# Expert blocks of 192 rows in a Mamba layer with a mixture of experts

## The chip, the core and the metric

The kernel runs on one core of a Trainium2 chip. A core has a matrix engine (TensorE, PE in the profile; its weight loads are listed as PEld), a vector engine (VectorE, DVE), an engine for activation functions (ScalarE, ACT), a general one (GpSimd, POOL), and SyncE (SP), which only issues transfers. They run beside each other and wait for each other through semaphores; 16 DMA engines move the data. Matrix products end in PSUM, which has eight banks of 512 fp32 columns by 128 partitions.

The metric is the time of one execution on the device in microseconds, lower is better. A profiled execution also leaves a trace, from which every duration below is taken.

## What is computed

4096 tokens of 256 numbers go through a Mamba layer, then through a layer in which each token is sent to one of eight experts. Both layers add their input and normalise. The second layer is what the change is about (`attn` stands for the first):

```python
x = _layernorm(x + attn(x, ...), axis=-1)
# D_MODEL, D_FF, N_EXP = 256, 1024, 8
logits = xf @ Wr.T + br
expert_idx = jnp.argmax(logits, axis=-1)
h = jax.nn.relu(jnp.einsum('td,efd->etf', xf, W1) + b1[:, None, :])
y = jnp.einsum('etf,edf->etd', h, W2) + b2[:, None, :]
out = y[expert_idx, jnp.arange(xf.shape[0])]
x = _layernorm(x + out, axis=-1)
```

The reference computes all experts for all tokens and picks one; the kernel computes only the expert that each token chose. All arithmetic of the two expert products is fp32.

## The kernel before

**Stages.** The Mamba layer runs over eight tiles of 512 tokens (`project`, `gauge`, `scan`, `gate`, `project_out`). `choose` and `rank` find each token's expert and its place in that expert's list, and `place` writes its number there (`lists`). The normalised tokens go to a DRAM array `x1d`, one row per token, with a row of zeros behind them.

**Expert blocks.** A block is up to 128 tokens of one expert's list. For block b, `prefetch` has POOL gather its tokens from `x1d` into `xg` (L399) and the expert's whole weights, 2.2 MB, into one of three buffers (L405, `held_weights[b % SLOTS]`), two blocks ahead (`AHEAD`). `turn` transposes the tokens on TensorE (L415), and DVE copies the result to `xgT` (L419). `hidden` computes the hidden layer in two halves, each of four chunks of 128 hidden units into one PSUM bank `ph` (L431); ACT empties the first half with bias and relu (L439), DVE the second (L441), both into `hT`. `close` computes the second product into one bank `pe` (L452), and calls `finish`: DVE adds tokens and bias (`xs`, L465) and the product (`r`, L467) and normalises (`layernorm`, L243 to L250; the square root in it is ACT's, L247). `scatter` has POOL write the rows to their tokens' places in `out` (L473). A row that stands for no token has an index beyond the end and isn't written.

**Tables.** Which expert and which tokens a block has is known only from the data. `table` computes it on DVE, with eight numbers per partition, one for each expert: `whole`, the rows that a list gives to the blocks of this table, then `ends` and `starts` of each list among the blocks, then for every block its place in `lists` (`row`, `pick`) and its expert (`eb`, `widx`). `lookup` fetches the tokens' numbers with a small product (`pi`) into `tidx`. Three early tables, after 3, 5 and 6 tiles, hand out 17 blocks that are full already; the last one, after all eight tiles, hands out the rest. In the last table the blocks are dealt to the three weight buffers in three runs, so that neighbours in a buffer often have the same expert; `same` then marks a load that isn't needed (its index goes out of bounds).

**How many blocks.** At most 39 are possible (`NSB`). `SURE` of them always run, here 37; the remaining two stand in a branch at the end (L940), entered on all engines when the last table's `total` exceeds the 20 blocks that are sure. The branch's condition is loaded into a register of every engine three blocks before the last (L931). Around the branch stand the scatters of the two blocks, from a tile `done` that is zeroed in case they do not run, and `finish` and `scatter` of block 36, which are kept behind it.

**Order.** TensorE's instructions run in the order in which the program writes them (`manual_schedule`, L109): the function `blocks` is a generator that yields after each quarter of a block, and the main loop calls `expert(n)` to run n quarters between the pieces of the Mamba layer. Blocks 0 to 10 or so lie among the last tiles; from then on only blocks run. The instructions of the other engines are ordered by the framework's scheduler, which may move an instruction ahead when what it needs is there. A branch is one unit in this order: on no engine do its instructions mix with others. PSUM's banks are dealt under three names: "mm" (three banks, `ph`), "o" (three, `pe`) and "tr" (two, the transposes).

Of the kernel before, what the change touches and what calls it, by code (L numbers as in the profile page):

```python
# [34 lines left out]
F32 = mybir.dt.float32  # L36
# [9 lines left out]
P = 128  # L46
# [3 lines left out]
TB = 512  # L50
# [11 lines left out]
SURE = 37  # L62
# [7 lines left out]
RUN = -(-(SURE - EARLY[6]) // SLOTS)  # L70
EPS = 1e-5
# [17 lines left out]
def mamba_moe(  # L89
# [148 lines left out]
    def layernorm(pool, rows, n, done, name):  # L238

        mv = pool.tile([P, n, 2], F32, tag="mv", name=f"mv{name}")  # L240
        for j in range(n):
            st = pool.tile([P, 6], F32, tag="st", name=f"st{name}_{j}")
            nc.vector.bn_stats(st, rows[:, j, :])  # L243
            nc.vector.bn_aggr(mv[:, j, :], st)
        sd = pool.tile([P, n], F32, tag="sd", name=f"sd{name}")
        nc.vector.tensor_scalar(sd, mv[:, :, 1], EPS, None, ALU.add)  # L246
        nc.scalar.activation(sd, sd, AF.Sqrt)  # L247
        nc.vector.reciprocal(sd, sd)
        for j in range(n):
            nc.vector.tensor_scalar(  # L250
                done[:, j, :], rows[:, j, :], mv[:, j, 0:1], sd[:, j : j + 1],
                ALU.subtract, ALU.mult,
            )
# [3 lines left out]
    index, weights = {}, {}  # L257
# [3 lines left out]
    held = []  # L261
    r1 = ctx.enter_context(tc.tile_pool(name="r1", bufs=1))
# [7 lines left out]
    def table(b0, nb, columns, rows, early):  # L270
# [5 lines left out]
        def wide(a):  # L276
            return a.unsqueeze(1).to_broadcast([P, nb, NE])
# [12 lines left out]
        nc.vector.tensor_tensor(whole, up, taken, ALU.subtract)  # L290
        ends = small("ends", [NE])
        nc.vector.tensor_tensor_scan(ends, ones8, whole, 0.0, ALU.mult, ALU.add)
        starts = small("starts", [NE])
# [9 lines left out]
        number = blockno[:, 0:nb].unsqueeze(2).to_broadcast([P, nb, NE])  # L303
        past = small("past", [nb, NE])
        nc.vector.tensor_tensor(past, wide(ends), number, ALU.is_le)
        here = small("here", [nb, NE])
        nc.vector.tensor_tensor(here, wide(starts), number, ALU.is_le)
        nc.vector.tensor_tensor(here, here, past, ALU.subtract)
        nc.vector.tensor_tensor(here, here, wide(shift), ALU.mult)
        row = small("row", [nb])  # L310
        nc.vector.tensor_reduce(row, here, AX.X, ALU.add)
        nc.vector.tensor_tensor(row, row, blockoff[:, 0:nb], ALU.add)
        pick = small("pick", [LH, nb])
# [3 lines left out]
        nc.vector.tensor_reduce(eb, past, AX.X, ALU.add)  # L317

        nc.vector.tensor_scalar(eb, eb, float(P), None, ALU.mult)
        if not early:  # L320

# [7 lines left out]
        for b in range(nb):  # L329
            weights[b0 + b] = widx[:, order(b0, b)]  # L330
# [661 lines left out]
```

## Time and profile before

Three runs took 503.46, 504.59 and 505.03 us, median 504.59. The execution that was profiled took 506.53 us, and its span, from the first to the last instruction in the trace, is 504.7 us. The granted TensorE clock averaged 0.995 of full speed.

| what | from the profile |
|---|---|
| hidden layer, L431 | 1184 instructions, 139.9 us busy |
| second product, L452 | 592 instructions, 135.0 us busy |
| transposes of tokens, L415 | 74 instructions, 14.2 us busy |
| evictions of the hidden layer | ACT L439 367 ns, DVE L441 343 ns each, 148 of each |
| one block's y from r on DVE and ACT | L467 423, L243 426, L244 181, L246 153, L247 203, L248 162, L250 433 ns |
| POOL, per issue | tokens L399 978 ns, weights L405 1048 ns, scatter L473 1028 ns |
| issue to landing, median | weights 9.2 us, tokens 4.7 us, scatter 7.1 us |
| engines from 461.97 to 469.22 us | PE 7.25, DVE 3.56, ACT 1.34, POOL 3.00 us busy of 7.25 |
| DMA in three stretches | 294 to 303 us: 381 GB/s; 310 to 346: 339; 418 to 491: 154 |

A fp32 matrix product is two instructions in the trace, so the 16 products of a block's hidden layer are 32. Their listed durations overlap, since matmuls are pipelined; what one really takes is seen in the distance between neighbours, or in the pieces of the chain of waits. That chain is followed back from the last instruction of the run, at each step to what released it; a piece is given as start, length, engine, tile, line and number of instructions. In the groups, "a | b | c" are the total busy time, and the idle time just before on that engine, with what ended most of it.

### The profile page before, as it was taken

How to read it: one execution, taken by the hardware profiler on the slowest of the kernel's cores; microseconds unless marked ns; L12 is line 12 of the kernel's file. 1: busy time of each engine (PE TensorE's matmuls, PEld its weight loads, DVE VectorE, ACT ScalarE, POOL GpSimd, SP SyncE). 2: the span in 40 equal slices, each digit the busy share in tenths (PEclk: the TensorE clock that was granted, in tenths of full speed). 3: DMA queues.
4: the chain of work that ended last, by engine and by line, in shares of the span. 5: the costliest groups of instructions: out<-in, count | busy, mean ns of one | idle time of the engine just before them, and what ended most of it. 6: DMA issues, size and time to landing. Idle time of an engine off the chain costs nothing.

```text
span 504.7 us, 7931 instructions
## 1 busy us (share of the span) xinstructions
PE 490.7 (97%) x2762; PEld 375.9 (74%) x2762; DVE 346.6 (69%) x1130; ACT 223.5 (44%) x472; POOL 184.5 (37%) x189
## 2 busy tenths in 40 slices
PE   7999999999999999999999999999999999999994
PEld 5444555545464586777889999999999999999994
DVE  2587869797999889869889785454545454545443
ACT  3786768777878774844351312211221222122211
POOL 2003022444446445323424233334433443344333
PEclk9998999999999999999999999999999999999999
DMA  7401012120408917507657598899755422811650
GB/s 239 142 1 43 0 43 83 44 83 0 127 1 354 340 29 258 189 0 269 227 202 266 220 359 312 330 363 342 276 201 205 158 97 55 346 54 33 222 192 22
DMA packets 23738, 84.89 MB, mean 168 GB/s; under 512 B 5934, under 2 KB 15665, under 8 KB 20242
## 3 DMA queue, kind: packets, MB, share of 16 engines
q0 software_dynamic: 9360, 69.60, 37.6%
q1 hardware_dynamic: 13378, 14.50, 9.1%
q8 instruction: 23, 0.38, 0.3%
q10 hardware_dynamic: 960, 0.27, 0.3%
q14 instruction: 17, 0.14, 0.1%
HBM read 102.75 MB, written 9.31 MB: 222 GB/s over the span
## 4 chain that ended last, share of the span: by engine, by line
PE 77%; DVE 14%; issue 3%; DMA 2%; ACT 2%; POOL 1%; POOLq 0%; SPq 0%; ACTq 0%
PE ph L431 26%; PE pe L452 25%; PE pm L526 12%; PE po L694 7%; DVE acc L539 5%; DVE cv L653 2%; PE pg L415 2%; PE px L561 2%; DMA xg<-x1d,tidx 1%; PE py L646 1%; DMA xTb<-in_xT 1%; PE pz L794 1%; DVE nma L712 1%; PE pt L620 1%; DVE sta L702 1%
## 5 line engine op out<-in xcount | busy, mean ns | idle before, releaser
L431 PEld LDWEIGHTS ph<-xgT,we 128*128 128x128 f32 x1184 | 138.5, 192 | 4.4 <-issue 1.1
L431 PE MATMUL ph<-xgT,we 128*128 128x128 f32 x1184 | 139.9, 275 | 0.0
L452 PE MATMUL pe<-we,hT 128*128 128x256 f32 x592 | 135.0, 379 | 0.0
L526 PE MATMUL pm<-xTb,win 128*128 128x512 f32 (+1 forms) x260 | 121.3, 597 | 1.3 <-DMA xTb<-in_xT 1.1
L452 PEld LDWEIGHTS pe<-we,hT 128*128 128x128 f32 x592 | 109.4, 190 | 13.6 <-DVE lg L735 0.3
L247 ACT ACTIVATE sdm<-sdm 128x1 f32<-128x1 f32 x37 | 7.5, 203 | 175.2 <-DVE sdm L246 175.2
L405 POOL DMA_INDIRECT we<-in_experts,widx x39 | 40.9, 1048 | 114.8 <-DVE r L467 82.5
L526 PEld LDWEIGHTS pm<-xTb,win 128*128 128x128 f32 x260 | 47.2, 191 | 47.7 <-issue 41.7
L539 DVE SCALAR_TENSOR_TENSOR acc<-xc,cw,acc 128x512 f32<-128x512 f32 x96 | 70.8, 766 | 16.8 <-ACT acc L535 16.4
L441 DVE TENSOR_SCALAR hT<-ph,we 128x128 f32<-128x128 f32 x148 | 42.6, 343 | 39.5 <-PE ph L431 39.5
L694 PE MATMUL po<-wout,sg 128*128 128x264 f32 x256 | 64.4, 393 | 1.3 <-DVE sg L658 1.3
L658 POOL TENSOR_TENSOR sg<-cv,sg 128x512 f32<-128x512 f32 x22 | 33.8, 1539 | 59.5 <-DVE cv L653 44.4
L694 PEld LDWEIGHTS po<-wout,sg 128*128 128x128 f32 x256 | 46.0, 190 | 11.7 <-issue 2.9
L467 DVE TENSOR_TENSOR r<-pe,xs 128x256 f32<-128x256 f32 x37 | 15.7, 423 | 53.2 <-PE pe L452 53.0
L473 POOL DMA_INDIRECT out<-y,tidx x37 | 38.0, 1028 | 38.4 <-DVE y L250 32.1
L399 POOL DMA_INDIRECT xg<-x1d,tidx x39 | 38.2, 978 | 37.6 <-DVE xs L465 9.6
L439 ACT ACTIVATE hT<-ph,we 128x128 f32<-128x128 f32 x148 | 42.1, 367 | 15.7 <-PE ph L431 13.2
L783 POOL TENSOR_SCALAR rowh<-lrow,row,code 128x256 f16<-128x256 bf16 x20 | 25.8, 1300 | 27.4 <-DVE row L775 27.4
L653 DVE SCALAR_TENSOR_TENSOR cv<-cv,dp,py 128x256 f32<-128x256 f32 x64 | 28.9, 470 | 2.4 <-PE py L646 2.4
L531 ACT ACTIVATE sg<-pm 128x512 f32<-128x512 f32 x32 | 19.0, 595 | 18.1 <-PE pm L526 15.8
L533 ACT COPY xc<-pm 128x512 f32<-128x512 f32 x32 | 18.6, 580 | 17.5 <-PE pm L526 17.4
L535 ACT ACTIVATE acc<-pm,cb,cw 128x512 f32<-128x512 f32 x32 | 25.1, 783 | 0.0
(156 smaller groups left out, 477.6 us busy)
## 6 DMA issues: line engine op xcount, KB each, us to landing
xb<-in_x SPq DMA_DIRECT2D x8, 512.0 KB, 4.9
x1d<-x SPq DMA_DIRECT2D x8, 512.0 KB, 5.0
xTb<-in_xT SPq DMA_DIRECT2D x7, 512.0 KB, 3.7
we<-in_experts,widx POOLq DMA_INDIRECT x39, 9.2
xg<-x1d,tidx POOLq DMA_INDIRECT x39, 4.7
out<-y,tidx POOLq DMA_INDIRECT x37, 7.1
win<-in_W_in SPq DMA_DIRECT2D x1, 512.0 KB, 5.7
we<-in_W_outT SPq DMA_DIRECT2D x1, 512.0 KB, 6.2
```

The lines of the kernel that those rows point to most:

```text
L399: nc.gpsimd.indirect_dma_start(out=xgs[n], out_offset=None, in_=x1d[0 : index[n][0], :], in_offset=bass.IndirectOffsetOnAxis(ap=index[n][1 ...
L405: nc.gpsimd.indirect_dma_start(out=wes[n][:, :], out_offset=None, in_=experts, in_offset=bass.IndirectOffsetOnAxis(ap=weights[n], axis=0), ...
L431: nc.tensor.matmul(ph[:, n * P : (n + 1) * P], lhsT=we[:, at : at + P], rhs=xgT[:, dc * P : (dc + 1) * P], start=(dc == 0), stop=(dc == DC ...
L439: nc.scalar.activation(hT[:, fc, :], ph[:, n * P : (n + 1) * P], AF.Relu, bias=bias)
L441: last[b] = nc.vector.tensor_scalar(hT[:, fc, :], ph[:, n * P : (n + 1) * P], bias, 0.0, ALU.add, ALU.max)
L452: nc.tensor.matmul(py[:, 0:D], lhsT=hT[:, fc, :], rhs=we[:, at : at + D], start=(fc == 0), stop=(fc == FC - 1),)
L473: moved = nc.gpsimd.indirect_dma_start(out=out, out_offset=bass.IndirectOffsetOnAxis(ap=index[b][1], axis=0), in_=ys[b][:, 0, :], in_offse ...
L526: nc.tensor.matmul(pm[:, at], lhsT=win[:, dc, c * P : (c + 1) * P], rhs=xTb[:, dc, at], start=(dc == 0), stop=(dc == DC - 1),)
L539: nc.vector.scalar_tensor_tensor(acc, xc[:, c, k : k + TB], cw[:, c, k : k + 1], acc, ALU.mult, ALU.add)
L653: nc.vector.scalar_tensor_tensor(cv[:, c, at], cv[:, c, at], dp[:, c : c + 1], py[:, 0 : TB // 2], ALU.mult, ALU.add,)
L658: eng.tensor_tensor(sg[:, c, :], cv[:, c, :], sg[:, c, :], ALU.mult)
L694: nc.tensor.matmul(po[:, 0 : D + NE], lhsT=sg[:, c, j * P : (j + 1) * P], rhs=wout[:, c, :], start=(c == 0), stop=(c == CC - 1),)
```

## The change

Block 17, 20, 23, 26 and 29, the blocks that one weight buffer gets from the last table, can hold 192 rows (`LONG`). The last table finds up to five experts whose lists end in 1 to 64 tokens beyond a multiple of 128 and have a full block before that; these tokens (`MORE`) go with the list's last full block, which is taken out of the ordinary order (`whole` loses two blocks) and put at the head of the table, where the long blocks are. With no such list, a long block runs as an ordinary one, with indices beyond the end in its further rows.

A long block has a second gather and a second scatter, two more transposes of 64 rows, a hidden layer of 192 columns in four PSUM banks of two chunks instead of two of four, a second product `pf` for the 64 further rows, whose even and odd chunks of hidden units go to two halves of a bank and are added by DVE, and a second `finish`. Its tiles lie in buffers of the Mamba layer that are free by then ("sg" and "xc").

32 blocks always run; the other seven stand in the branch, which moves from the end to between blocks 29 and 30 (`BRANCH`, `seldom`). Their tokens are gathered before the branch, their rows scattered after it, whether it is entered or not. Inside, each of them has its weights loaded by SP into one buffer. Block 30 is turned after the branch instead of during block 29, and block 31's `finish` is no longer held back.

```diff
-SURE = 37
+SURE = 32
...
 RUN = -(-(SURE - EARLY[6]) // SLOTS)
+EXTRA, MORE = 5, 64
+LONG = {EARLY[6] + SLOTS * n: n for n in range(EXTRA)}
+BRANCH = SURE - 2
...
+    def layernorm(pool, rows, done, name):
+
+        n = rows.shape[0]
+        st = pool.tile([P, 6], F32, tag="st", name=f"st{name}")[0:n, :]
+        nc.vector.bn_stats(st, rows)
+        mv = pool.tile([P, 2], F32, tag="mv", name=f"mv{name}")[0:n, :]
+        nc.vector.bn_aggr(mv, st)
+        sd = pool.tile([P, 1], F32, tag="sd", name=f"sd{name}")[0:n, :]
+        nc.vector.tensor_scalar(sd, mv[:, 1:2], EPS, None, ALU.add)
...
+        longer = 0 if early else EXTRA
+        if longer:
+
+            low = small("low", [NE], I32)
+            nc.vector.tensor_scalar(low, pn[:, 0:NE], float(MORE - 1), None, ALU.add)
+            nc.vector.tensor_scalar(low, low, -P, None, ALU.bitwise_and)
+            more = small("more", [NE])
+            nc.vector.tensor_tensor(more, up, low, ALU.subtract)
+            nth = small("nth", [NE])
+            nc.vector.tensor_tensor(nth, low, taken, ALU.is_gt)
+            nc.vector.tensor_tensor(more, more, nth, ALU.mult)
+
+            nc.vector.tensor_tensor_scan(nth, ones8, more, 0.0, ALU.mult, ALU.add)
+            nc.vector.scalar_tensor_tensor(
+                more, nth, float(longer * P), more, ALU.is_le, ALU.mult
+            )
+            nc.vector.tensor_tensor(nth, nth, more, ALU.subtract)
+            base = small("base", [1])
+            nc.vector.tensor_reduce(base, more, AX.X, ALU.add)
+            nc.vector.scalar_tensor_tensor(whole, more, -2.0, whole, ALU.mult, ALU.add)
+
+            key = small("key", [NE])
+            nc.vector.tensor_scalar(key, more, 0.0, float(OFF), ALU.is_equal, ALU.mult)
+            nc.vector.tensor_tensor(key, key, nth, ALU.add)
+            mine = small("mine", [longer, NE])
...
+            row_of = small("row_of", [longer])
+            nc.vector.tensor_reduce(row_of, mine, AX.X, ALU.add)
         ends = small("ends", [NE])
         nc.vector.tensor_tensor_scan(ends, ones8, whole, 0.0, ALU.mult, ALU.add)
+        if longer:
+            nc.vector.tensor_scalar(ends, ends, base, None, ALU.add)
...
+        row = small("row", [nb + longer])
+        nc.vector.tensor_reduce(row[:, 0:nb], here, AX.X, ALU.add)
+        if longer:
+            nc.vector.tensor_tensor(row[:, 0:longer], row[:, 0:longer], row_of, ALU.add)
+            nc.vector.scalar_tensor_tensor(
+                row[:, nb:], row_of, float(P), blockoff[:, 0:longer], ALU.add, ALU.add
...
+            nc.vector.tensor_scalar(
+                spare, eb[0:1, SURE - b0 : NSB - b0], float((NE - 1) * P), None, ALU.min
+            )
...
+            for b, x in LONG.items() if longer else ():
+                further[b] = tidx[0:MORE, nb + x : nb + x + 1]
...
     def prefetch(b):
-        for n in range(b, min(b + AHEAD, NSB - 1) + 1):
+        for n in range(b, min(b + AHEAD, SURE - 1) + 1):
             if n in index and n not in xgs:
                 xgs[n] = m3.tile([P, D], F32, tag="xg", name=f"xg{n}", bufs=4)
-                nc.gpsimd.indirect_dma_start(
-                    out=xgs[n], out_offset=None, in_=x1d[0 : index[n][0], :],
-                    in_offset=bass.IndirectOffsetOnAxis(ap=index[n][1], axis=0),
-                )
+                gather(xgs[n], *index[n])
+                if n in LONG:
+                    ends_[n] = a2.tile([P, CC, KC - 1 + TB], F32, tag="xc", name=f"long{n}")
+                    ends_[n] = ends_[n].rearrange("p c t -> p (c t)")
+                    xgf[n] = ends_[n][0:MORE, 0:D]
+                    gather(xgf[n], index[n][0], further[n])
...
+    def rows_of(b):
+        return P + MORE if b in LONG else P
+
+    def buffer(b):
+
+        if b not in wide_:
+            wide_[b] = a3.tile([P, CC, TB], F32, tag="sg", name=f"wide{b}")
+            wide_[b] = wide_[b].rearrange("p c t -> p (c t)")
+        return wide_[b]
+
     def turn(b):
 
+        n = rows_of(b)
         px = bank("tr", f"pg{b}", 2)
         for dc in range(DC):
-            nc.tensor.transpose(
-                px[:, dc * P : (dc + 1) * P], xgs[b][:, dc * P : (dc + 1) * P], ident
-            )
-        turned[b] = m2.tile([P, DC * P], F32, tag="xgT", name=f"xgT{b}")
-        nc.vector.tensor_copy(turned[b], px[:, 0 : DC * P])
+            at = slice(dc * P, (dc + 1) * P)
+            nc.tensor.transpose(px[:, dc * n : dc * n + P], xgs[b][:, at], ident)
+            if b in LONG:
+                nc.tensor.transpose(
+                    px[:, dc * n + P : (dc + 1) * n], xgf[b][:, at], ident[0:MORE, 0:MORE]
+                )
+        if b in LONG or b >= SURE:
+            turned[b] = buffer(b)[:, FC * n : (FC + DC) * n]
+        else:
+            turned[b] = m2.tile([P, DC * P], F32, tag="xgT", name=f"xgT{b}")
+        nc.vector.tensor_copy(turned[b], px[:, 0 : DC * n])
...
+        per = 512 // P if b not in LONG else 2
+        for first in range(half * FC // 2, (half + 1) * FC // 2, per):
+            ph = bank("mm", f"ph{b}_{first}")
+            for n in range(per):
+                for dc in range(DC):
+                    at = dc * FF + (first + n) * P
+                    nc.tensor.matmul(
+                        ph[:, n * w : (n + 1) * w], lhsT=we[:, at : at + P],
+                        rhs=xgT[:, dc * w : (dc + 1) * w],
+                        start=(dc == 0), stop=(dc == DC - 1),
+                    )
...
-        if half == 0 or b == SURE - 1:
+        if half == 0:
             return
+        if b in LONG:
+
+            openf[b] = bank("o", f"pf{b}")
+            for fc in range(FC):
+                g = fc % 2 * MORE
+                nc.tensor.matmul(
+                    openf[b][g : g + MORE, 0:D], lhsT=hT[:, fc, P:], rhs=out_weights(fc),
+                    start=(fc < 2), stop=(fc >= FC - 2), tile_position=(0, g),
+                )
         finish(b)
...
+        layernorm(m2, r, ys[b], f"m{b}")
+        if b in LONG:
+            xs, r, yf[b] = (ends_[b][0:MORE, n * D : (n + 1) * D] for n in (1, 2, 3))
+            nc.vector.tensor_tensor(xs, xgf[b], we[0:MORE, OC : OC + D], ALU.add)
+            for g in range(2):
+                part_sum = openf[b][g * MORE : (g + 1) * MORE, 0:D]
+                nc.vector.tensor_tensor(r, part_sum, r if g else xs, ALU.add)
+            layernorm(m2, r, yf[b], f"f{b}")
...
+        for rows, at in ((ys[b], index[b][1]), *(((yf[b], further[b]),) if b in LONG else ())):
+            moved = nc.gpsimd.indirect_dma_start(
+                out=out, out_offset=bass.IndirectOffsetOnAxis(ap=at, axis=0),
+                in_=rows, in_offset=None, bounds_check=T - 1, oob_is_err=False,
+            )
...
+    def seldom():
+
+        rows = a3.tile([P, CC, TB], F32, tag="cv", name="rows").rearrange("p c t -> p (c t)")
+        for b in range(SURE, NSB):
+            xgs[b] = ys[b] = rows[:, (b - SURE) * D : (b - SURE + 1) * D]
+            gather(xgs[b], *index[b])
+        with tc.If(held[1] > (SURE - EARLY[6]) * P, preferred_fallthrough_block=False):
+            for b in range(SURE, NSB):
+                wes[b] = held_weights[(BRANCH - 1) % SLOTS]
+                row = nc.values_load(
+                    spare[0:1, b - SURE : b - SURE + 1], engines=[mybir.EngineType.SP],
+                    min_val=0, max_val=(NE - 1) * P,
+                )
+                nc.sync.dma_start(wes[b], experts[bass.ds(row, P), :])
+                turn(b)
+                for half in range(2):
+                    hidden(b, half)
+                for half in range(2):
+                    close(b, half)
...
+        for b in range(SURE):
             current = b
+            if b == BRANCH:
+                seldom()
...
-            if 0 < b < SURE:
+            if 0 < b:
                 scatter(b - 1)
+            if b == BRANCH:
+                for n in range(SURE, NSB):
+                    scatter(n)
             if b not in turned:
                 turn(b)
...
-            if b + 1 in xgs and b + 1 < SURE:
+            if b + 1 in xgs and b + 1 not in (BRANCH, SURE):
                 turn(b + 1)
...
-        if current == SURE - 3 and len(held) == 1:
+        if current == BRANCH - 3 and len(held) == 1:
...
-    done = a2.tile([P, NSB - SURE, D], F32, tag="xb", name="done")
-    nc.vector.memset(done, 0.0)
-    for b in range(SURE, NSB):
-        ys[b] = done[:, b - SURE : b - SURE + 1, :]
-    with tc.If(held[1] > (SURE - EARLY[6]) * P, preferred_fallthrough_block=False):
-        for _ in blocks(SURE, NSB):
-            pass
-    for b in range(SURE, NSB):
-        scatter(b)
-
-    finish(SURE - 1)
     scatter(SURE - 1)
```
`gather` issues the indirect transfer that `prefetch` wrote out before. `mine` and `expert_of`, left out above with three more lines of the table, say which expert a long block has; `hid` of a long block is the first part of `buffer(b)`, and `w` is `rows_of(b)`.

## Prediction

> **What bounds the kernel now.** I read the summary of the page first, then the chain of waits over the last two hundred microseconds, then single blocks in it, and last the timeline of the end.
>
> ```profile
> PE 490.7 (97%) x2762; PEld 375.9 (74%) x2762; DVE 346.6 (69%) x1130; ACT 223.5 (44%) x472; POOL 184.5 (37%) x189
> ...
> PEclk9998999999999999999999999999999999999999
> ```
>
> TensorE is busy nearly all the time at its full clock; DVE is only half used in the last 200 us. A busy share alone does not prove a bound, so the chain of waits between 346 and 360 us is the real evidence:
>
> ```profile
> 346.21 3.57 PE ph L431 x32
> 349.79 0.22 PE pg L415 x2
> 350.00 3.46 PE pe L452 x16
> 353.46 3.57 PE ph L431 x32
> ```
>
> The pieces abut: 3.57 + 0.22 + 3.46 = 7.25 us, and the next block starts at 353.46. No piece of another engine stands between them from 283 us to the last matmul. This expert stage is bound by TensorE alone, so a block less is worth its whole 7.25 us, and a column more costs what TensorE takes for it. Weight loads do not set the pace here: a load is issued at most once per block, lands in 9.2 us (median), and is asked for two blocks (14.5 us) ahead.
>
> **Removed: five blocks.** The loop that always runs goes from 37 to 32. 5 x 7.25 = **-36.2 us**.
>
> **Added: five blocks grow to 192 rows.** Four terms for each, all on TensorE.
> - *Hidden layer.* 32 instructions (an fp32 product is two) now stream 192 columns. For 128 columns one takes 3.57/32 = 0.1116 us; for 256 columns (the second product) 3.46/16 = 0.216 us; for 512 columns (pm, 1.72 us for 4) 0.430 us. The three lie on a line, so 192 columns is the middle of the first two, 0.164 us: 32 x 0.0523 = +1.67 us.
> - *Second product of the 64 further rows (pf).* 16 instructions of 256 columns, in two column groups of 64 (`tile_position`). Unpaired they would cost 3.46 us. The nearest row uses the same two groups:
>
> ```profile
> 192.74 1.72 PE pm L526 x4
> 194.45 1.87 PE px L561 x8
> 196.32 1.98 PE ph L431 x16
> ```
>
> Eight px instructions of 512 columns take 1.87 us where four full-width ones take 1.72, so the groups run beside each other. pf is the same number of streamed columns in twice as many instructions: +1.87 us. Here a rule speaks against the change. The Trainium skill, TensorEngine Tiling (Array Packing), says under Key Properties that a change of tiling mode drains TensorE, and under Restrictions that column tiling switches fast weight load off. If each of the 16 weight loads (137 ns in the px row) stood bare beside 16 x 0.108 us of streaming, pf would be about 3.9 us and the five blocks 10 us dearer. The px row leaves only 1.87 - 1.72 = 0.15 us for drain and loads together, so I take the row; it has half as many loads per column, which is why I keep 3.9 as the upper end.
> - *Transposes.* Two more, of 64 rows; two of 128 take 0.22 us. Between 0.11 and 0.22; I take 0.15.
>
> Sum 3.69 us for a long block, 5 x 3.69 = **+18.5 us**. Net of the two parts: **-17.8 us** (between -19 and -8).
>
> The other work of a long block lies beside TensorE. DVE gets one more sum chain (about 3 us) in a stretch where it works 3.56 of 7.25 us; the chain follows pf and must be through before the next block's L441, which is 3.57 us into that block: it fits. ACT's evictions are 4 x 0.37 us before and little wider now. The four ph banks of a long block rotate through three; the first is emptied 1.5 us before it is needed. POOL issues two more transfers (2 x 1.3 us with their gap); it idles 3.2 us in every block. If one of these covers failed, the cost would be under 1 us a block.
>
> **The last table.** About 24 small DVE instructions of 0.15 to 0.2 us are added, at most 4.8 us of chain. In the trace `pick` is done at 300.16 us (L315), and TensorE takes it up at 305.92 (pi): 5.8 us of cover. The evictions L441 that alternate with the table have 1.3 us of slack before their matmul. I take **0**; without the cover up to +2. The table's tokens are needed only at block 17, which begins near 347 us, 40 us after tidx.
>
> **The branch moves into the stream.** Before, it stands after TensorE's last product and hides there. Now it stands between blocks 29 and 30, and block 29 is a long one. What counts is the DVE queue: all of block 29's ends are before the branch, and `turn(30)`, which is no longer done ahead, is behind it. TensorE cannot start block 30 until DVE has copied xgT. With E as the end of block 29's pe: the chain for one block is read at the end of the trace,
>
> ```profile
> 498.18 0.42 DVE L467 TENSOR_TENSOR r<-pe,xs 128x256 f32<-128x256 f32 x1 [1.49 <-PE pe L452]
> ...
> 499.94 0.41 DVE L250 TENSOR_SCALAR y<-r,mvm,sdm 128x256 f32<-128x256 f32 x1
> ```
>
> that is 2.17 us from r to the end of y, with matmuls ended at 498.14. So block 29's own y is done at E + 2.2; its further rows need one more addition (0.46) and the same chain (2.17): E + 4.9. The branch itself:
>
> ```profile
> L940 DVEq COMPARE_BRANCH  x2: 51/53/55, 494.7 to 496.0; - x2
> ...
> L940 PEldq COMPARE_BRANCH  x2: 95/202/310, 495.9 to 498.3; - x2
> ...
>   DVE xs L465: 0.4, 1
> ```
>
> DVE loses 0.4 us; then xgT 0.41, the hop to TensorE and its first weights 0.2: E + 5.9. TensorE alone would go on at E + 1.87 (after pf) plus 0.22 for the transposes. A gap of **+3.8 us**. TensorE's own branch (0.31 us after its drain, at E + 2) and its transposes are over by E + 3 and lie inside the gap. Lower end 1 us, if the chain of the further rows turns out to run beside something; upper end 7.5.
>
> The upper end comes from a second rule. The Trainium skill, Runtime: NRT & Kernel Launch, Instruction fetch mechanics, says that a taken branch to a target outside the fetched window waits for a DMA of the target page. In the trace the branch jumped past two blocks and the next PE event came within 0.1 us, so no such wait is seen; now seven blocks (some 700 TensorE instructions) lie in between, while the instruction queue's packets are 0.38 MB / 23 = 16.5 KB each. The nearest price is a small transfer's landing, 3.6 us (al, 0.1 KB). On TensorE (ready at about E + 6.5 with xgT then still to come) it would add 1 us; on DVE all 3.6. DVE's body is about 90 instructions, so I take the row, not the rule: no fetch wait.
>
> POOL gathers seven unused blocks' rows before the branch (7 x 1.26 = 8.8 us) and scatters them after it (9 us more). Nothing keeps the gathers from being placed early, into POOL's 3.2 us idle per block, as the memset `done` was (written at the end of the program, run at 272 us). The scatters have 17 us until the last one. Cost **0**; if the gathers are left in a row in front of the branch, from 3.7 us into block 29 on, the last lands 12.5 us later (11.5 us to issue it, 4.7 to land), near E + 7.5, and if the branch's body is waited for, the gap is 6.8 instead of 3.8 us.
>
> SP's, ACT's and the other engines' register loads for the branch move with it (block 27 instead of 34); in the trace TensorE's load at 476.0 us left its period at 7.25. Cost 0. **The end** keeps its form: from the last pe to the end of the span 504.7 - 498.14 = 6.6 us before and after.
>
> **Sum.** -36.2 + 18.5 + 3.8 = -13.9 us. The profiled execution took 506.53 us with a span of 504.7; it would become 492.6 (span 490.8). The shown runs' median, 504.59, lies 1.9 us under that execution, so the forecast for a median is 504.59 - 13.9 = **490.7 us**.
>
> **Rivals.**
> 1. *The gap at the branch is larger* (page fetch, or gathers in front of the branch, or both): +3 to +7 on the sum, 493.5 to 498. For it: 8.8 us of POOL work and a body 3.5 times longer. Against it: slack on POOL and the cheap branch in the trace. 0.22.
> 2. *pf does not pair*, 3.5 to 3.9 us instead of 1.87: 5 x 1.6 to 2.0 us, 499 to 500.7. For it the rule; against it the px row. 0.05.
> 3. *No gap at the branch*: -17.8 + about 1, 487 to 488. For it: nothing but that DVE might be ordered more cleverly. 0.08.
> 4. *Slower: the branch is taken*, and the change does not do what it says. It decides at more than 15 blocks in the last table. Each of seven further blocks then costs 7.25 us, and its weights, all in one buffer and loaded after the block before, 9.2 more: 7 x 16.4 = 115 us, about 606 us. Against it: I counted the reference's choices for its inputs, 495, 560, 487, 548, 514, 589, 514 and 389 tokens. That is 37 blocks of 128; 17 are done early, 20 are left; five lists end in 1 to 64 tokens (48, 36, 2, 2, 5) and each saves one: exactly 15. There is no block to spare, but no list stands where one token changes it for the worse. 0.05, with all other ways to end slower.
>
> The forecast itself, 488.5 to 493.5, has 0.60. The range takes rivals 1 and 3 in: 487 to 497. The measurement tells some 0.3% (1.5 us) from no change. Faster 0.93, the same 0.02, slower 0.05.
>
> **What would show it.** ph as x1024 in two shapes: 32 x 27 of 128 columns and 32 x 5 of 192, the chain giving 5.24 us for 32 of the latter; pf x80 in five pieces of about 1.9 us; blocks 7.25 us and long ones 10.9; one hole in TensorE between block 29 and 30 of about 3.8 us that ends on DVE xgT, with DVE's L250 just before the branch. The forecast is wrong if the hole ends on a DMA or on nothing seen (a fetch), if pf takes over 2.5 us, or if TensorE has holes elsewhere.

## The result, and the profile after

The changed kernel takes **497.89 us** (median of five runs, 496.98 to 499.94) against 504.24 of the kernel before (503.31 to 505.03). The ratio is 0.9886, with a 95% interval of 0.9854 to 0.9917: faster by 1.1%, or 6.3 us. Forecast were 13.9 us less, 490.7, with a range that ended at 497.0. The branch was not taken: 32 blocks ran. Less than half of the expected gain arrived. From here on, "before" and "after" are the two kernels, and e1 to e12 the experiments.

From the page of after:

```profile
PE 478.5 (97%) x2602; PEld 357.9 (72%) x2602; DVE 343.8 (69%) x1133; ACT 218.6 (44%) x452; POOL 187.2 (38%) x193
...
PEclk9999999999999999999999999999999999999979
```

Two things stand out. TensorE's clock falls in the last but one slice, where before it was full until the end. And TensorE lost only 12 us of busy time, where the forecast took away 17.8 (five blocks less, five longer ones).

The profiled executions took 506.53 us before and 497.31 after, 9.2 us apart, more than the medians. Three of these come from before the changed part: block 16's first ph starts at 343.22 us after, and before at 346.05 (timeline; the chain in the prediction puts it 0.16 later):

```profile
346.05 3.73 PE L431 MATMUL ph<-xgT,we 128*128 128x128 f32 x32
```

The same work starts between 343.2 and 347.5 us in the traces of this study. So I count from there: 158.7 us to the end of the span before, 152.1 after, **6.6 us less**, close to the 6.3 of the medians.

The timeline of after, TensorE alone (start, length, engine and line, operation, tiles, form, number; in brackets the idle time before and what ended it), at the first long block, 17, and at the branch:

```profile
343.22 3.73 PE L526 MATMUL ph<-xgT,we 128*128 128x128 f32 x32
346.79 0.27 PE L500 MATMUL pg<-ident,xg 128*128 128x128 f32 x1
346.99 0.27 PE L502 MATMUL pg<-ident,long 64*128 64x64 f32 x1
347.19 0.33 PE L500 MATMUL pg<-ident,xg 128*128 128x128 f32 x1
347.45 0.27 PE L502 MATMUL pg<-ident,long 64*128 64x64 f32 x1
347.65 3.72 PE L551 MATMUL pe<-we,hT 128*128 128x256 f32 x16
351.21 5.36 PE L526 MATMUL ph<-wide,we 128*128 128x192 f32 x32
356.41 0.38 PE L500 MATMUL pg<-ident,xg 128*128 128x128 f32 x2
356.63 3.62 PE L551 MATMUL pe<-we,wide 128*128 128x256 f32 x16
360.18 1.95 PE L562 MATMUL pf<-we,wide 128*64 128x256 f32 x16
362.06 3.84 PE L526 MATMUL ph<-xgT,we 128*128 128x128 f32 x32
...
465.47 1.95 PE L562 MATMUL pf<-we,wide 128*64 128x256 f32 x16
471.25 0.66 PE L500 MATMUL pg<-ident,xg 128*128 128x128 f32 x2 [3.83 <-DVEq L603]
472.47 5.78 PE L526 MATMUL ph<-xgT,we 128*128 128x128 f32 x32 [0.56 <-issue]
478.09 0.38 PE L500 MATMUL pg<-ident,xg 128*128 128x128 f32 x2
```

Read the distances between starts, not the lengths. The 192-column hidden layer takes 356.41 - 351.21 = 5.20 us and pf 362.06 - 360.18 = 1.88: both as forecast. But the four transposes take 347.65 - 346.79 = 0.86 us. At the branch TensorE stands from the end of pf (467.4) to 472.47, but for the two transposes, and then block 30's hidden layer takes 478.09 - 472.47 = 5.62 us instead of 3.57. Busy times of this layer in two stretches (PE, PEld, DVE, ACT, POOL, then the granted clock, the DMA share, GB/s) show the clock at half and then at full:

```profile
472.50:476.40 3.90, 3.90 (x17) 3.79 (x18) 0.00 (x0) 0.00 (x0) 2.98 (x4) 0.50 0.02 0
476.40:478.10 1.70, 1.70 (x18) 1.70 (x17) 0.00 (x0) 1.14 (x4) 1.12 (x2) 1.00 0.05 10
```

The branch itself, from the view of its line:

```profile
L603 PEldq COMPARE_BRANCH  x2: 95/1781/3467, 465.5 to 467.6; - x2
...
L603 DVEq COMPARE_BRANCH  x2: 51/53/55, 469.8 to 470.7; - x2
```

TensorE's second branch instruction, 0.31 us in the kernel before, is 3.47 us long (the three numbers are minimum, median and maximum in ns). It starts at 467.6 and so ends at 471.1, just before the transposes. (Their line names DVE's queue as what ended their wait; but DVE is past its branches at 470.8.) DVE's branches are as short as before.

One hole more, at block 26, on TensorE and DVE:

```profile
428.70 1.99 PE L551 MATMUL pe<-we,hT 128*128 128x256 f32 x8 [0.48 <-DVE hT L537]
```

```profile
427.64 0.42 DVE L581 TENSOR_TENSOR long<-long,we 64x256 f32<-64x256 f32 x1 [3.93 <-DMA we<-in_experts,widx]
```

DVE stood 3.9 us before L581, the addition of tokens and bias for block 26's further rows, which needs block 26's weights; block 25's evictions waited behind it.

The 6.6 us in stages, forecast beside trace:

| stage | forecast | measured, and from what |
|---|---|---|
| five blocks less | -36.2 | -36.2, 7.25 a block |
| five long blocks | +18.5 | +22.2: three blocks with a long one 26.19 (351.21 to 377.40) less 3 x 7.25, times 5 |
| hole at block 26 | 0 | +0.7: that step 8.74 (421.79 to 430.53), in others 8.00 |
| gap at the branch | +3.8 | +4.9: 467.4 to 472.47, less 0.2 for the transposes |
| block 30 at a lower clock | 0 | +2.05: 5.62 against 3.57 |
| end | 0 | -0.2 |
| sum | -13.9 | -6.55 |

### The profile page after: what moved, and what is told of

Its sections match the earlier page's. It is cut to its first block, busy times and chain, and to the rows that moved or that the text cites. A ratio compares the mean times of both kernels' runs of the same rounds, so it can differ in the third digit from the quotient of the medians.

```text
span 495.3 us, 7570 instructions
## 1 busy us (share of the span) xinstructions
PE 478.5 (97%) x2602; PEld 357.9 (72%) x2602; DVE 343.8 (69%) x1133; ACT 218.6 (44%) x452; POOL 187.2 (38%) x193
## 5 line engine op out<-in xcount | busy, mean ns | idle before, releaser
L526 PEld LDWEIGHTS ph<-xgT,we 128*128 128x128 f32 x864 | 102.6, 195 | 6.7 <-issue 2.1
L526 PE MATMUL ph<-xgT,we 128*128 128x128 f32 x864 | 105.0, 279 | 0.9 <-issue 0.6
L551 PE MATMUL pe<-we,hT 128*128 128x256 f32 x432 | 100.1, 382 | 0.5 <-DVE hT L537 0.5
L551 PEld LDWEIGHTS pe<-we,hT 128*128 128x128 f32 x432 | 79.4, 190 | 12.0 <-DVE hT L537 1.7
L478 POOL DMA_INDIRECT we<-in_experts,widx x32 | 33.8, 1058 | 89.2 <-DVE r L575 50.4
L535 ACT ACTIVATE hT<-ph,we 128x128 f32<-128x128 f32 x108 | 31.2, 366 | 34.0 <-PE ph L526 24.0
L537 DVE TENSOR_SCALAR hT<-ph,we 128x128 f32<-128x128 f32 x108 | 31.2, 341 | 21.2 <-PE ph L526 21.1
L461 POOL DMA_INDIRECT xg<-x1d,tidx x32 | 32.1, 1003 | 32.1 <-DVE xs L573 6.6
L526 PE MATMUL ph<-wide,we 128*128 128x192 f32 x160 | 26.8, 326 | 0.0
L526 PEld LDWEIGHTS ph<-wide,we 128*128 128x128 f32 x160 | 26.3, 190 | 0.3
```

Source lines behind the costliest of these rows:

```text
L461: nc.gpsimd.indirect_dma_start(out=to, out_offset=None, in_=x1d[0:rows, :], in_offset=bass.IndirectOffsetOnAxis(ap=at, axis=0),)
L478: nc.gpsimd.indirect_dma_start(out=wes[n][:, :], out_offset=None, in_=experts, in_offset=bass.IndirectOffsetOnAxis(ap=weights[n], axis=0), ...
L526: nc.tensor.matmul(ph[:, n * w : (n + 1) * w], lhsT=we[:, at : at + P], rhs=xgT[:, dc * w : (dc + 1) * w], start=(dc == 0), stop=(dc == DC ...
L535: nc.scalar.activation(hT[:, fc, :], ph[:, n * w : (n + 1) * w], AF.Relu, bias=bias)
L537: last[b] = nc.vector.tensor_scalar(hT[:, fc, :], ph[:, n * w : (n + 1) * w], bias, 0.0, ALU.add, ALU.max)
L551: nc.tensor.matmul(py[:, 0:D], lhsT=hT[:, fc, 0:P], rhs=out_weights(fc), start=(fc == 0), stop=(fc == FC - 1),)
```

## Experiments

The times of all kernels include the first 343 us, which differ by several microseconds between the traces: the framework orders the other engines' work anew in each build, and executions of one build differ too (503 to 507 us before). So a verdict on a part is read in the stage, and the ratio to the kernel before is given beside it.

**e1, block 30 turned ahead; e2, a short jump; e3, both.**

```diff
-            if b + 1 in xgs and b + 1 not in (BRANCH, SURE):     # e1, e3
+            if b + 1 in xgs and b + 1 != SURE:
...
-            for b in range(SURE, NSB):                           # e2, e3
+            for b in range(SURE, SURE + 2):
```

> Block 30 is turned during block 29 again, the branch stays as it is. In the changed kernel TensorE stands 5.1 us between the end of pf and the first ph of block 30, and its branch instruction is 3.47 us long. Theory (the jump over seven blocks waits for its instructions): the gap stays near 3.9 us (0.2 drain, 3.5 branch, 0.2 restart), it ends on TensorE's own branch, and the time falls by 1 to 2 us, to about 496.5. Rival (the prediction's: DVE's queue holds block 30's xgT back): with xgT ready before, the gap is at most 0.7 us and the time falls by 6 to 7 us, to about 491.

> The branch's body holds two of the seven seldom blocks, as many as before the change; the other five blocks' work is left out. Theory (the jump's distance sets the wait): TensorE's branch takes 0.3 us instead of 3.47, the gap before block 30 is then ended by DVE's xgT, about 4.0 us instead of 5.1, and the time falls by about 1 us; how much of block 30's slow hidden layer (5.8 instead of 3.6 us) stays depends on whether a gap of 4 us still lowers the clock. Rival (the branch itself is long, whatever the distance): branch 3.5 us, gap 5.1, no change.

> Both edits: block 30 turned during block 29, and a body of two of the seven seldom blocks (the other five are left out). Theory (two waits lie beside each other in the gap, the fetch and DVE's queue, and the lost clock follows the gap): only now the gap goes, to 0.5 to 0.8 us; block 30's hidden layer takes 3.6 us again at the full clock; the time falls by 6 to 7 us, to about 491.3. Rival (the slow hidden layer of block 30 has another cause than the gap): it stays at 5.8 us and the time falls by 4.4 us.

| | median | ratio to before | TensorE's long branch | pf to first ph of block 30 | its hidden layer |
|---|---|---|---|---|---|
| after | 497.89 | 0.9886 (0.9854 to 0.9917) | 3.47 | 5.1 | 5.6 |
| e1 | 499.65 | 0.9905 (0.9886 to 0.9925) | 3.62 | 4.1 | 8.3, a hole of 2.2 in it |
| e2 | 496.35 | 0.9847 (0.9794 to 0.9900) | 0.19 | 4.1 | 5.1 |
| e3 | 495.82 | 0.9815 (0.9773 to 0.9858) | 0.19 | 3.0 | 5.3 |

e1, TensorE's timeline:

```profile
467.76 1.95 PE L562 MATMUL pf<-we,wide 128*64 128x256 f32 x16
473.70 1.13 PE L526 MATMUL ph<-xgT,we 128*128 128x128 f32 x8 [3.99 <-issue]
477.03 5.12 PE L526 MATMUL ph<-xgT,we 128*128 128x128 f32 x24 [2.20 <-issue]
```

With xgT ready, TensorE still stands 4.1 us, as the theory had it, and it starts when its own branch is over. "issue" is a wait for nothing that the profile shows. Eight matmuls on, it stands again for 2.2 us in the same way. e1 gained nothing.

e2 and e3: with the body of two blocks the branch takes 0.19 us. So its length follows the size of the body that is jumped over. That TensorE waits there for its instructions is supported by the DMA view: between 467.6 and 471.1 us, the time of the branch in after, the queue for instructions moves one packet, of 16 KB,

```profile
q8 instruction: 1, 0.02, 1.9%
```

and in the same stretch of e2 none. The traces of all eight branches over seven blocks, 3.3 to 3.8 us long, have such a packet inside the branch; none of those over two blocks has (before, e2, e3, e5; 0.19 to 0.31 us). In e1 one more moves at 474.2 us, in front of the second wait; no run tested that one.

The gap of e2 is then ended by DVE's queue, 4.1 us less 0.2 for the transposes, 3.9: the 3.8 of the forecast. It came by another path, though. The forecast had the transposes over early in the gap; here they too wait until DVE is at the branch, and DVE waits for them before it copies xgT:

```profile
470.38 0.41 PE L500 MATMUL pg<-ident,xg 128*128 128x128 f32 x2 [2.99 <-DVEq L603]
```

That e3 would have no gap and take 491.3 us was wrong. Its line of the branch, and TensorE behind it:

```profile
L603 DVEq COMPARE_BRANCH  x2: 51/53/55, 471.3 to 471.8; - x2
```

```profile
471.79 5.47 PE L526 MATMUL ph<-xgT,we 128*128 128x128 f32 x32 [2.96 <-DVEq L603]
```

xgT was there long before; TensorE starts at 471.79, the moment in which DVE passes the branch's end. A branch works as a meeting point here: the first matmul behind it waits until DVE has gone past, which it does only after block 29's two sums. So three waits lay in one gap: for DVE to pass (3.0 us after pf, e3), for the transposes and their copy behind that (4.1, e2), and for the fetch (4.1, e1; 5.1 with the transposes behind it, after). Taking one away uncovered the next.

**e4, no branch.** The If and its body are taken out, block 30 is turned ahead.

> No branch at all: the seven seldom blocks' work is left out, their gathers and scatters stay, block 30 is turned during block 29. This is the whole price of the branch in the stream: theory 7.1 us (5.1 us of gap less 0.2 for the transposes, 2.2 for the clock), so about 490.8 us; what then still differs from the forecast without a gap (486.9) is the price of the long blocks, about 4 us.

490.56 us, ratio 0.9727 (0.9686 to 0.9767), as expected. Block 30 starts at 466.83, right behind pf of block 29 at 464.95, and the clock is full throughout. From block 16 to the end it takes 144.5 us against 152.1. The branch in the stream costs 7 of these 7.6 us; the rest is the hole at block 26, which is not in this trace.

**e5, TensorE kept busy in the gap.** As e3, with 24 transposes of the identity into a spare bank between pf and the branch.

```diff
+                fill = bank("tr", "fill", 2)
+                for n in range(24):
+                    nc.tensor.transpose(fill[:, n % 4 * P : (n % 4 + 1) * P], ident, ident)
                 seldom()
```

> As e3 (two seldom blocks in the branch, five left out; block 30 turned ahead), and TensorE runs 24 transposes of the identity into a spare bank (about 2.6 us) between pf of block 29 and the branch, which nobody reads. In e3 block 30's first matmul starts 3.0 us after pf, when DVE has passed the branch, and its hidden layer takes 5.3 us at a lowered clock. Theory (idle time on TensorE lowers its clock): the start stays where it was against pf, the idle gap shrinks to some 0.5 us, the hidden layer takes 3.6 us and the whole is about 1.7 us faster than e3, though TensorE does more. Rival (block 30 is slow because of something the branch leaves behind, as instructions fetched late): 5.3 us again, and no gain.

Busy times in two stretches each of e3 and of e5: the gap or the filled gap, then block 30's hidden layer.

```profile
469.00:471.80 2.80, 0.01 (x1) 0.01 (x1) 2.20 (x8) 0.20 (x1) 0.97 (x1) 1.00 0.15 50
471.80:477.10 5.30, 5.30 (x33) 5.30 (x34) 0.00 (x0) 1.14 (x4) 2.87 (x3) 0.68 0.03 4
```

```profile
470.60:473.20 2.60, 2.60 (x26) 2.56 (x24) 2.15 (x8) 0.20 (x1) 0.97 (x1) 1.00 0.15 51
474.10:477.80 3.70, 3.67 (x33) 3.70 (x34) 0.00 (x0) 1.14 (x4) 2.60 (x3) 1.00 0.04 8
```

The same 32 instructions run at a clock of 0.68 in 5.3 us and at 1.00 in 3.6 us (0.68 is a mean: in e3 too the clock is 0.50 until 475.3 us and 1.00 from there). So idleness is what slows block 30, not what the branch leaves behind. From the end of pf to the end of that layer e5 is 1.1 us faster than e3 (7.2 against 8.3), since the fill was a little long and TensorE's branch came after it. The whole is not: 497.37 us, 0.9859 (0.9804 to 0.9913). In its trace TensorE stands 1.18 and 1.15 us in blocks 24 and 27, each time for an eviction on ACT (L535) which comes 3 us late; the kernels e6 to e8, run beside it, show the same two holes, the others don't. What ACT waited for there stays open.

**e6, the branch behind everything; e7 and e8, the transposes, on top of e6.** In e6 `seldom()` comes after block 31's scatter, and the seldom blocks' scatters are inside the branch.

```diff
             nc.tensor.transpose(px[:, dc * n : dc * n + P], xgs[b][:, at], ident)     # e7
-            if b in LONG:
+        for dc in range(DC if b in LONG else 0):
+            at = slice(dc * P, (dc + 1) * P)
...
-                nc.tensor.transpose(                                                   # e8
-                    px[:, dc * n + P : (dc + 1) * n], xgf[b][:, at], ident[0:MORE, 0:MORE]
+                nc.tensor.matmul(
+                    px[:, dc * n + P : (dc + 1) * n], lhsT=ends_[b][:, at],
+                    rhs=ident[:, 0:MORE], start=True, stop=True,
```

> The branch with all seven blocks stands behind everything, after block 31's scatter; the seldom blocks' rows are scattered inside the branch; block 30 is turned ahead. Theory (the price of the branch is a price of its place in TensorE's stream): the gap before block 30 is gone, all blocks run at the full clock, and the time is that of e4 without a branch, 490.5 us, plus at most 1.5 us. Rival (engines wait for one another at the branch and the fetch of 3.5 us delays the end): 493.5 us or more.

> As e6, and a long block's two transposes of 128 rows come first, then its two of 64 rows. In the changed kernel the four alternate and take 0.86 us, against 0.22 for two and an estimate of 0.15 more. Theory (each change between a 128-row and a 64-row tile drains TensorE, about 0.15 us): two changes are left of four, 0.55 us for the four, 5 x 0.3 = 1.5 us less than e6. Rival (a transpose of 64 rows is slow in itself): 0.86 us still, time of e6.

> As e6, and the 64 further rows are turned as full 128-row products with 64 identity columns (the rows beyond are zeroed first), so no tile of 64 rows occurs among the transposes. Theory (the change of tile is what costs): the four take about 0.4 us instead of 0.86, 5 x 0.45 = 2.3 us less than e6, about 488.3. Rival (the weights of further rows cost what they cost): no change.

e6: 501.36 us, 0.9946 (0.9929 to 0.9964), slower than after, where 492 at most was expected. The gap before block 30 is gone and the clock is full, but the end is 13.8 us long instead of 6.3 (from the last pe, 485.2, to 499.0). Two lines of its trace, the branch's and the program's last:

```profile
L603 POOLq INC_SWDGE_SEM  x1: 2419/2419/2419, 481.0 to 481.0; - x1
```

```profile
L1114 POOLq DRAIN  x3: 45/113/10523, 487.6 to 498.7; - x3
```

The first is an instruction that the branches without POOL's transfers don't have; it lies beside TensorE's last products and delays nothing. The second is what makes the end long: POOL's last drain takes 10.5 us, in after 3.1, and in e12, whose branch stands at the end too but has no transfers of POOL in it, 5.1. TensorE's own branch is over at 488.9. So POOL's transfers inside a branch are not free when it isn't taken; why the drain takes so long stays open.

e7 and e8, against e6, in the step from one hidden layer to the next long one: e6 344.34 to 352.33, 7.99 us; e7 345.46 to 353.16, 7.70; e8 344.94 to 352.58, 7.64. The four transposes take 0.86, 0.58 and 0.56. Same work, two changes of size instead of four: 0.29 us less, so a change costs about 0.15, as an estimate. With none, e8 still takes 0.56 where 0.4 was expected; its products are two instructions each, and what else is in the rest was not tried. As totals, 500.08 (0.9909, 0.9878 to 0.9941) and 501.12 (0.9937, 0.9921 to 0.9953); e8's gain of 5 x 0.35 us does not show in it.

**e9, skipped rows; e10, the addition behind the eviction.** Both on the changed kernel.

```diff
-            gather(xgs[b], *index[b])                                          # e9
+            nc.gpsimd.indirect_dma_start(
+                out=xgs[b], out_offset=None, in_=x1d[0 : index[b][0], :],
+                in_offset=bass.IndirectOffsetOnAxis(ap=index[b][1], axis=0),
+                bounds_check=T - 1, oob_is_err=False,
+            )
...
-            nc.vector.tensor_tensor(xs, xgf[b], we[0:MORE, OC : OC + D], ALU.add)   # e10
+            with tc.issue_after(last[b].ins):
+                nc.vector.tensor_tensor(xs, xgf[b], we[0:MORE, OC : OC + D], ALU.add)
```

> As the changed kernel, but the gathers of the seven seldom blocks skip the rows that stand for no token (index beyond the last token; the tile is zeroed once) instead of reading the one row of zeros 128 times each. In the changed kernel three such gathers at 412 to 415 us fill the DMA engines (share 1.0 at 60 to 100 GB/s until 419 us), the weights issued behind them land at 427.6, DVE waits for them with an addition of block 26, and TensorE stands 0.5 us at 428.7. Theory (many reads of one row are slow and hold the weights back): no stretch of full DMA share under 120 GB/s, DVE's wait at that place under 1.5 us instead of 3.9, no hole in TensorE before block 26; 0.5 to 1 us faster. Rival (POOL's four microseconds of issuing hold the weights back): DVE's wait stays over 3 us.

> As the changed kernel, but the addition of tokens and bias for a long block's further rows is kept behind the same block's last eviction on DVE, as the ordinary one is. Theory (DVE's queue stops at this addition, which waits for the weights of a block whose turn has not come): the wait for a DMA on DVE goes, y of the block before is done in its usual time, no hole in TensorE before block 26; 0.5 to 1 us faster. Rival (the weights are late for TensorE too): the hole stays, it then ends on a DMA.

Stretches of 1 us behind three such gathers, after first, then e9:

```profile
415.00:416.00 1.00, 1.00 (x12) 1.00 (x11) 0.93 (x3) 0.00 (x0) 0.70 (x2) 1.00 1.02 102
416.00:417.00 1.00, 1.00 (x12) 1.00 (x11) 0.40 (x3) 0.43 (x3) 0.70 (x1) 1.00 0.78 61
417.00:418.00 1.00, 1.00 (x12) 1.00 (x10) 0.56 (x2) 0.79 (x4) 1.00 (x1) 1.00 1.08 66
```

```profile
416.00:417.00 1.00, 1.00 (x10) 0.91 (x9) 0.93 (x4) 0.00 (x0) 0.78 (x1) 1.00 0.03 1
417.00:418.00 1.00, 1.00 (x12) 1.00 (x11) 0.92 (x3) 0.00 (x0) 0.69 (x2) 1.00 0.03 1
```

In after the DMA engines' share is 0.8 to 1.1 and they move 60 to 100 GB/s; from 409 to 412 us the same share moves 436 to 453. 128 reads of one row of DRAM, three times, occupy them for microseconds; skipped, they occupy nothing. (An ordinary gather, of 128 different rows, left them at a share of 0.37 from 430 to 431 us; three of those in a row were not tried.) The hole before block 26 is gone in e9: from block 16 to block 29 it takes 112.75 us (344.88 to 457.63) against 113.50 (343.22 to 456.72). The expectation for DVE was too good, its wait is still 2.6 us. In e10 DVE's wait at the addition is gone, the weights are as late as in after (their last packet ends 84 us after the start of block 16 in both, 82 in e9), and the hole is gone as well: 112.76 us. So both were needed for the hole, late weights and an addition that stops DVE's queue for them. It is a narrow matter: e1 to e4 have neither repair, their DVE waits 3.3 to 3.6 us at this place, and they have no hole; only the 3.9 of after reached TensorE. So the missing hole proves little in e9, where the wait of 2.6 is what counts; in e10 weights as late as those of after made none. As totals, 499.00 and 499.02, both 0.9867: 0.7 us is less than what builds differ by.

**e11 and e12, together.** Both have the repairs of e8, e9 and e10. e11 has no branch; e12 has all of it, behind the last pe, with block 31's sum and scatter after it.

> No branch (the seldom blocks' work left out), block 30 turned ahead, and the three repairs together: skipped rows in the seldom gathers, the addition behind the eviction, and further rows turned as full products of 128 rows. Theory (these and the branch are all that the forecast missed): e4's 490.6 less 1.75 for the transposes and up to 1 for the stalls, 487.5 to 489, no hole in TensorE from block 11 to the end. Rival (something else is in the long blocks): 490 or more.

> A whole version: the three repairs, and the branch with all seven blocks after block 31's last product, as the kernel before has it (the seldom blocks' second product goes to a bank of the other name, their scatters follow the branch, then block 31's sum and scatter). Theory: TensorE's fetch is off the path, seven empty scatters on POOL (9 us) stand before the last one and cost 3 to 4 us, so 491 to 493 us, 4 to 6 us faster than the changed kernel. Rival (engines wait for one another at the branch at the end as well): 495 or more.

e11: 491.58 us, 0.9732 (0.9696 to 0.9768), no faster than e4 (490.56) as a whole, and the rival's number. In the stage the forecast holds: no hole, and 142.8 us from block 16 to the end, 1.7 less than e4. But block 16 starts at 347.5 us instead of 343.2. Two of the repairs zero buffers on DVE, and the framework put the first of these among the last tiles of the Mamba layer (172.9 us); that this is the cause was not tried by itself.

e12: 496.64 us (494.56 to 497.38), ratio 0.9825 (0.9797 to 0.9853). Its interval lies below that of after, so it beats both kernels, by less than hoped, and the total is the rival's number. From block 16 to the end it takes 148.0 us (346.92 to 494.9), 4.1 less than after: in the stage the forecast of 4 to 6 holds. Its end:

```profile
482.06 0.97 POOL L592 DMA_INDIRECT out<-rows,tidx  x1 [1.60 <-DVEq L611]
...
491.02 0.98 POOL L592 DMA_INDIRECT out<-y,tidx  x1 [0.30 <-issue]
```

y of block 31 is done at 486.2 (L259), its scatter starts at 491.0, behind seven scatters of rows that don't exist, with which POOL could begin only when DVE had passed the branch (1.60 us). That is 4.5 us, a little over the 3 to 4 expected; most of the rest of the distance to the expected 491 to 493 is again before block 16. A hole of 0.44 us before block 26 is back as well, though the repairs of e9 and e10 are in:

```profile
430.25 0.27 DVE L474 MEMSET long<- 64x256 f32 x1 [3.41 <-DMA out<-long,tidx]
```

This time DVE's queue stops at the zeroing that e8's repair brought in, which waits for an earlier scatter to land.

## Why the prediction was wrong

Two terms of the sum failed. The branch was put at +3.8 us and cost 7.0: the fetch behind the jump was put at nothing, on the word of a shorter jump, and the clock was no term at all. The long blocks were put at +18.5 and cost 22.2: the changes between 128 and 64 rows or columns were put at nothing.

- **Five blocks less, -36.2; TensorE as the bound.** Right to 0.1 us. (The chain of waits leaves TensorE at 494.70, within the last block, and not at the last matmul; no term rested on that.)
- **Hidden layer of 192 columns, +1.67; pf, +1.87.** Right: 1.63 and 1.88. Column groups run beside each other, and the row of px stood for pf. The rule weighed there, of a drain at each change of tiling mode (the Trainium skill, TensorEngine Tiling (Array Packing), Key Properties), was put aside for pf, where it costs some 0.1 us at each end. The row itself held that cost: the ph piece behind px takes 1.98 us for 16 instructions, where 3.57/2 = 1.79 was due and the one at 279.34 us, with no such change before it, takes 1.78. I read px and not what followed it.
- **Transposes, +0.15.** Wrong, +0.64. The rule applied here and I didn't ask: four transposes alternate between 128 and 64 rows. The row "two for 0.22 us" has no change in it. With 0.3 us at the ends of pf and of the transposes this is 3.8 us over five blocks, half of what was missed. e7 halves the changes and gets 0.29 us back.
- **The branch, +3.8.** Wrong as a whole, 7.0. The term that I priced, DVE's queue, had the right size: e2 shows 3.9. In part that is luck, since the transposes waited for DVE at the branch, which the forecast didn't have. Two more were not in the sum. *The fetch* lay beside DVE's wait and ended some 0.8 us later (transposes at 471.25, in e2 at 470.38, with pf at the same time), and the gap was 1.0 us longer; I had the rule (the Trainium skill, Runtime: NRT & Kernel Launch, Instruction fetch mechanics) and took the trace of a short jump over it, though the jump was to become three and a half times as long. e2 settles the price: 0.19 us over two blocks, 3.5 over seven. *The clock*: after the idle time TensorE runs at half its clock for most of one hidden layer, +2.05 us, which e5 shows to come of the idleness. The Trainium skill, TensorE: Matmul & The Clock Gate, What's actually happening, says that an idle window of about 3.4 us halves the clock, and that the windows run freely; the trace of before had no such gap in its last half, but I forecast one of 3.8 us and didn't ask what follows from it. Here 3.0 us were enough (e3).
- **POOL's gathers, 0.** Right for POOL, wrong for the DMA engines, which I did not look at: one row read 128 times. With DVE's early addition, which I had taken to be free, 0.7 us, and not in each execution traced.
- **The last table, 0; the end, 0.** Right: no hole in TensorE at the table, and 6.3 us from the last pe to the end.
- **Rivals.** The second wait at the branch (0.22 for "the gap is larger") is what came, joined by the clock and the transposes, which stood in no rival.

## What to carry to other kernels

Price a branch by what every engine does on both sides of it: a jump past a long body waits for its instructions, the first work behind it can wait for the slowest engine to pass, and a gap of three to five microseconds on TensorE cost 1.5 to 2.7 more in clock. A duration read in a trace belongs to its neighbours too: an instruction between others of the same shape says nothing on one that alternates with another shape, and a short jump says nothing on a long one. When each of several waits ends at nearly the same time, removing one shows the next, so take them away in pairs before a cause is named.

## What the runs showed of the hardware

- The jump over a branch's body took TensorE 0.19 to 0.31 us past two blocks and 3.3 to 3.8 past seven, with a packet of the instruction queue inside each long one; in one build a second wait of 2.2 us followed eight matmuls later.
- After 3.0 us without work TensorE's granted clock averaged 0.68 over the next 5.3 us (0.50, then 1.00); after 0.7 us it stayed at 1.00.
- Two 64-row transposes alternating with two of 128 rows: 0.86 us for the four, 0.58 when sorted.
- Gathers of one and the same DRAM row filled the DMA engines at 60 to 100 GB/s, where a full share otherwise moves about 430 to 450.
- POOL's indirect transfers inside a branch that isn't taken, at the end of the program, went with an end 7.5 us longer (e6).
